# The exponentials' scores of an attention kernel: twelve products of 32 and 2 rows, or four products of 72 rows

## The chip, the cores and the metric

One core of a Trainium2 chip. The metric is device time in microseconds (us) of one launch: 1179.71 in the median of three runs (1178.32 to 1181.1). Lower is better.

## The reference, cut to what matters

One transformer layer on x of shape 2 x 1024 x 512: layer norm, attention with 32 heads of 16 columns, residual, layer norm, a feed-forward net (FFN) with ternary weights and rounded inputs, residual. The change concerns the scores and the softmax.

```python
q, k, v = (proj(w_q), proj(w_k), proj(w_v))        # (2, 32, 1024, 16) each
scores = jnp.einsum('bhqd,bhkd->bhqk', q, k) / jnp.sqrt(jnp.float32(D_K))
attn = jax.nn.softmax(scores, axis=-1)             # exp(scores - max over k) / sum
out = jnp.einsum('bhqk,bhkd->bhqd', attn, v)
```

All inputs are float32. The softmax subtracts each query's maximum, so the kernel forms the scores twice: once with queries on the partitions, to take the maximum along the keys, and once with keys on the partitions, to take the exponential and multiply with v.

## The kernel before, in words

**Steps and slots.** The attention is cut into 32 steps: batch b (2), half of the queries h (2, 512 each), group g of eight heads (4), and s (2), which picks every other head of the group. So a step has four heads (r = 0 to 3) and 512 queries. A step's maxima take eight slots (512 keys x 128 queries of all four heads each), its exponentials eight others (128 keys x 512 queries), its product with v eight (128 keys each). The main loop (L1400 to L1445) runs over slots T. In slot T stand the maxima of step T/8, the exponentials of the step that began LE = 10 slots earlier, and the product with v of the exponentials of one slot earlier. TensorE, VectorE, ScalarE, GpSimd and SyncE each work through their own instructions in the order in which this loop writes them.

**Numbers in two halves.** q and k are each split into a part hi that TensorE multiplies exactly and a rest lo. A tile kst of 128 rows holds for each of the four heads 32 rows: 16 of hi, 16 of lo. qst is a pair of tiles: in qst[0] both 16-row halves are q's hi, in qst[1] its lo. One product of 32 rows (kst with qst[0]) adds hi*hi and lo*hi, a second one (with qst[1]) the rest. Each head has its own quarter of TensorE's rows, so products of different heads can run at once.

**Maxima.** max_mm (L586) makes 8 such products a slot, two for each head, into two score tiles (psm, 128 x 1024 in PSUM, two heads each). max_reduce (L598) has VectorE reduce each of them to two columns of pm. After a step's last slot max_parts (L602) joins the parts on VectorE and splits the negative maximum into hi and lo columns of mcols; max_rows (L610) turns them into rows with four small products (psn) and ScalarE copies them to mrow (L617), in the second slot of the next step.

**Exponentials.** exp_mm (L621) makes for each head two products of 32 rows with kst and qst, and a third of 2 rows, ones against the maximum's two rows in mrow, that subtracts the maximum. That is 12 a slot. exponentials (L632) has ScalarE take exp of each score tile of two heads (pse) into e.

**The order in a slot.** scores (L637) interleaves the exponentials of one pair of heads with the maxima of the other pair, so that all four quarters of the rows are in use: ten products in a run. The slot is: mixed run; product with v (weigh_values, L655: for each head 128 keys x 32 columns against e, accumulated in pso over the step); short fill; second mixed run; max_rows if due; fill.

**Fills.** Everything else (layer norm, projections, output projection, FFN, quantization of the FFN's weights) are generators in a planner (class Fillers, L31). Each slot it runs those that are due, by costs written in the code (L1444), mostly one or two groups of matrix products. Tasks of kind "back" (normalise, L671; weight sums, L757; weight quantization, L796) advance one step at each call, two a slot.

**Buffers.** Score tiles come from one PSUM pool of three (ps_s), given out in turn: two maxima tiles and two exponential tiles a slot, and psn's. The product with v has a bank of its own, the fills another. In SBUF kst has three buffers, qst six (three pairs), e four.

**Transfers.** project_qk (L460) writes hi and lo of q and k to DRAM (qD, kD), in the layout that lets load_k and load_q (L566, L569) read a step's kst (512 KB) and qst (2 x 256 KB) five slots before the step's maxima. load_v (L575) reads v (512 KB). For the first two steps parts of kst and qst are copied from SBUF directly (L492 to L506) and q is not written to DRAM. Nearly all of these are issued on SyncE's queue, in order; the weights' raw loads (load_raw, L750) on GpSimd's.

**The end** (the_end, L1043) is the last quarter's output projection and FFN, in an order of its own, in tiles that are free by then.

```python
def exp_mm(n, i, j, ps, l):
    for r in (2 * j, 2 * j + 1):
        rows = slice(32 * r, 32 * r + 32)
        if l < 2:
            left, right = kst[n][rows, i * P : (i + 1) * P], qst[n][l][rows, :]
        else:
            rows = slice(32 * r, 32 * r + 2)
            left, right = onesr[rows, :], mrow[n][rows, :]
        nc.tensor.matmul(ps[:, r % 2, :], left, right, start=(l == 0), stop=(l == 2))
```

## Time and profile before

| | us |
|---|---|
| median of three runs | 1179.71 |
| lowest and highest run | 1178.32, 1181.1 |
| span of the profiled execution | 1179.7 |
| ScalarE, exponentials (L634), 512 of 1.023 | 522.7 |
| VectorE, reductions of the maxima (L600), 512 of 1.222 | 623.8 |
| TensorE, maxima (L590), 2048 | 369.5 |
| TensorE, exponentials' scores (L630), 2048 of 32 rows, 1024 of 2 | 367.6 + 203.9 |
| TensorE, product with v (L660), 2048 | 272.9 |
| data moved | 135.35 MB, mean 115 GB/s |

The times of lines are those of the page's costliest groups. On TensorE a group's time is the stretch in which it and no earlier product ran, since products overlap; so the place of a run is better read from the starts in the timeline. The product with v and other float32 products appear as two records each. The chain of work that ended last lies on TensorE for 81% of the span, with 25% on the exponentials' scores, 18% on the product with v and 9% on the maxima. DMA engines are busy 50 to 70% of the time in the first 320 us and mostly 20 to 40% later.

### The profile page before, as it was taken

How to read it: one execution, taken by the hardware profiler on the slowest of the kernel's cores; microseconds unless marked ns; L12 is line 12 of the kernel's file. 1: busy time of each engine (PE TensorE's matmuls, PEld its weight loads, DVE VectorE, ACT ScalarE, POOL GpSimd, SP SyncE). 2: the span in 40 equal slices, each digit the busy share in tenths (PEclk: the TensorE clock that was granted, in tenths of full speed). 3: DMA queues.
4: the chain of work that ended last, by engine and by line, in shares of the span. 5: the costliest groups of instructions: out<-in, count | busy, mean ns of one | idle time of the engine just before them, and what ended most of it. 6: DMA issues, size and time to landing. Idle time of an engine off the chain costs nothing.

```text
span 1179.7 us, 21990 instructions
## 1 busy us (share of the span) xinstructions
PE 1154.8 (98%) x8922; PEld 522.5 (44%) x8922; DVE 868.8 (74%) x1261; ACT 686.8 (58%) x878; POOL 264.1 (22%) x319
## 2 busy tenths in 40 slices
PE   8899999999999999999999999999999999999998
PEld 5454444544444444544444445444444433444344
DVE  6765577898876677788866665786988788888467
ACT  2058765556565556566665555465666555665746
POOL 3224336465501101221011011022110001220111
PEclk9999999999999999999999999999999999999999
DMA  5666765556623323443633324244442516362300
GB/s 157 174 183 194 249 197 176 172 190 197 194 93 96 103 55 110 113 95 77 94 86 121 124 59 147 84 130 138 84 97 60 89 53 83 58 81 55 79 9 37
DMA packets 97099, 135.35 MB, mean 115 GB/s; under 512 B 34829, under 2 KB 54285, under 8 KB 96997
## 3 DMA queue, kind: packets, MB, share of 16 engines
q1 hardware_dynamic: 87204, 105.75, 34.6%
q0 software_dynamic: 9792, 28.19, 7.7%
q8 instruction: 70, 1.15, 0.4%
q14 instruction: 33, 0.26, 0.1%
HBM read 89.25 MB, written 37.19 MB: 107 GB/s over the span
## 4 chain that ended last, share of the span: by engine, by line
PE 81%; DVE 5%; DMA 5%; issue 2%; POOL 2%; SPq 2%; ACT 2%; POOLq 0%; DVEq 0%; ACTq 0%
PE pse L630 25%; PE pso L660 18%; PE psm L590 9%; PE psv L533 4%; PE psk L476 4%; PE psy L847 4%; PE psq L476 4%; PE pu L937 2%; PE py L1006 2%; DVE pm L600 2%; PE pg L937 2%; DMA rden<-rD 1%; PE psn L613 1%; SPq L505 1%; PE end L1161 1%
## 5 line engine op out<-in xcount | busy, mean ns | idle before, releaser
L600 DVE TENSOR_REDUCE pm<-psm 128x2 f32<-128x1024 f32 x512 | 623.8, 1222 | 242.9 <-PE pse L630 146.0
L634 ACT ACTIVATE e<-pse 128x1024 f32<-128x1024 f32 x512 | 522.7, 1023 | 408.2 <-PE pse L630 307.3
L590 PE MATMUL psm<-kst,qst 32*128 32x512 f32 x2048 | 369.5, 444 | 7.3 <-DMA kst<-kD 3.8
L630 PE MATMUL pse<-qst,kst 32*128 32x512 f32 x2048 | 367.6, 442 | 3.9 <-DVE pm L600 3.1
L630 PEld LDWEIGHTS pse<-qst,kst 32*128 32x128 f32 x2048 | 149.2, 183 | 332.8 <-issue 199.7
L660 PE MATMUL pso<-e,v 128*32 128x512 f32 x2048 | 272.9, 605 | 0.0
L630 PE MATMUL pse<-mrow,onesr 2*128 2x512 f32 x1024 | 203.9, 396 | 0.0
L590 PEld LDWEIGHTS psm<-kst,qst 32*128 32x128 f32 x2048 | 151.3, 183 | 25.5 <-ACT e L634 10.8
L630 PEld LDWEIGHTS pse<-mrow,onesr 2*128 2x128 f32 x1024 | 94.5, 183 | 3.3
L951 POOL TENSOR_TENSOR g<-g 128x460 f32<-128x460 f32 (+1 forms) x36 | 34.7, 964 | 244.7 <-ACT g L947 237.4
L660 PEld LDWEIGHTS pso<-e,v 128*32 128x32 f32 x2048 | 40.4, 108 | 94.4 <-issue 93.7
L807 POOL TENSOR_SCALAR low<-raws,whalf 128x512 bf16<-128x512 f32 (+2 forms) x35 | 52.0, 1488 | 30.5 <-DMA raws<-in_wuT 8.1
L476 PE MATMUL psq<-xnT,wq 128*128 128x512 f32 x112 | 57.8, 626 | 0.0
L533 PE MATMUL psv<-wv,xnT 128*128 128x128 f32 x384 | 53.2, 285 | 0.0
L533 PEld LDWEIGHTS psv<-wv,xnT 128*128 128x128 f32 x384 | 45.9, 191 | 12.5 <-issue 11.7
L847 PE MATMUL psy<-wo,OT 128*128 128x512 f32 x96 | 49.6, 625 | 0.0
L476 PE MATMUL psk<-xnT,wk 128*128 128x512 f32 x96 | 49.5, 624 | 0.0
L699 POOL TENSOR_TENSOR OT<-po,rden 128x512 f32<-128x512 f32 x15 | 19.2, 1278 | 99.5 <-PE pse L630 52.8
L547 POOL DMA_DIRECT2D vD<-vst x30 | 16.7, 559 | 110.5 <-ACT vst L545 107.8
L909 POOL TENSOR_SCALAR xn<-x,mv,a 128x512 f32<-128x512 f32 x12 | 25.1, 2089 | 71.5 <-DVE a L885 71.5
L937 PEld LDWEIGHTS <-xqT 128*128 128x128 bf16 x288 | 22.4, 98 | 37.8 <-issue 23.8
L937 PE MATMUL pg<-wg,xqT 128*128 128x460 fp8e4 (+1 forms) x144 | 34.2, 360 | 0.0
(227 smaller groups left out, 945.1 us busy)
## 6 DMA issues: line engine op xcount, KB each, us to landing
v<-vD SPq DMA_DIRECT2D x32, 512.0 KB
kst<-kD SPq DMA_DIRECT2D x31, 512.0 KB
qst<-qD SPq DMA_DIRECT2D x60, 256.0 KB
vD<-vst POOLq DMA_DIRECT2D x30, 256.0 KB, 5.7
qD<-hi_q SPq DMA_DIRECT2D x28, 256.0 KB
qD<-lo_q SPq DMA_DIRECT2D x28, 256.0 KB
x<-in_x SPq DMA_DIRECT2D x20, 256.0 KB
rden<-rD SPq DMA_DIRECT2D x15, 256.0 KB
```

Source lines behind the costliest of these rows:

```text
L476: nc.tensor.matmul(ps, w[:, c, :], xnT[b, h][:, c, :], start=(c == 0), stop=(c == KC - 1))
L533: nc.tensor.matmul(ps[:, i * P : (i + 1) * P], xnT[b, half][:, c, i * P : (i + 1) * P], w[:, c, :], start=(c == 0), stop=(c == KC - 1),)
L590: nc.tensor.matmul(ps[:, r % 2, :], qst[n][l][rows, t * P : (t + 1) * P], kst[n][rows, kh * QB : (kh + 1) * QB], start=(l == 0), stop=(l = ...
L600: nc.vector.tensor_reduce(pm[n][:, t, kh, 2 * j : 2 * j + 2], ps, AX.X, ALU.max, negate=True)
L630: nc.tensor.matmul(ps[:, r % 2, :], left, right, start=(l == 0), stop=(l == 2))
L634: nc.scalar.activation(e, ps, AF.Exp, scale=SCALE)
L660: nc.tensor.matmul(acc[n][32 * r : 32 * r + 32, :], vt[n][:, i, r, :], e[r // 2][:, r % 2, :], start=(i == 0), stop=(i == NT - 1),)
L807: nc.gpsimd.tensor_scalar(low, w, h[:rows, m, 1:2], None, ALU.is_lt)
L847: nc.tensor.matmul(ps, OT[b, h, g][:, i * P : (i + 1) * P], wo[g], start=(g == 0), stop=(g == NG - 1),)
L909: nc.gpsimd.tensor_scalar(xn, xt, mean, a, ALU.subtract, ALU.mult)
L937: nc.tensor.matmul(ps, xT[:, c, :], w[:, c, n : n + size], start=(c == 0), stop=(c == KC - 1))
L951: nc.gpsimd.tensor_tensor(g2[j], g2[j], g2[j], ALU.mult)
```

## The change

The exponentials' scores of a head become one product. A tile kw of 72 rows holds for each head 64 rows of k (hi and lo, each twice) and 8 rows of zeros and ones; qm holds 64 rows of q (hi, hi, lo, lo in the order that pairs each with each) and 8 rows with the maxima of all four heads, of which the ones in kw pick the two of the head. So one product over 72 of the 128 rows gives a head's scores with the maximum subtracted; a slot has four, on the whole array, one after another.

Two tiles kw hold four slots of keys each; load_kw reads one (512 KB) four slots before its use. load_qm reads qm (512 KB) for a step while its maxima are formed. kD holds k's rows twice (each half of k is written with four transfers, not two), and the first q is written to qD as well. The maxima's rows go into qm: ScalarE copies 8 rows x 2048, one copy for each head side by side.

The order in a slot: the maxima of all four heads in one run; product with v; short fill; the exponentials' four products; fill; then max_rows, in the first slot of the next step and not the second.

To make room, kst has two buffers, qst four, e two, mcols one, and the raw weights and their helper tile use the FFN's tiles; two gaps in normalise are longer; the_end takes its tiles from other buffers.

```diff
--- before
+++ after
@@ -311,10 +307,10 @@
-    mcols = [const.tile([P, TQ, P], F32R, name=f"mcols{k}") for k in range(2)]
+    MROW = 64
+    mcols = const.tile([P, TQ, P], F32R, name="mcols")
     vst = [const.tile([P, 2, 4, 4, 32], F32, name=f"vst{k}") for k in range(1)]
-    for m in mcols:
-        nc.gpsimd.memset(m.bitcast(F32), 0.0)
+    nc.gpsimd.memset(mcols.bitcast(F32), 0.0)
     for v in vst:
@@ -413,12 +409,12 @@
     qD = {
-        (b, g, h): dram.tile([2, 8 * 32, QB], F32, name=f"qD_{b}_{g}_{h}")
+        (b, g, h): dram.tile([8 * 64, QB], F32, name=f"qD_{b}_{g}_{h}")
         for b in range(B)
     }
-    kD = {(b, g): dram.tile([8 * 32, S], F32, name=f"kD_{b}_{g}") for b in range(B) for g in range(NG)}
+    kD = {(b, g): dram.tile([8 * 64, S], F32, name=f"kD_{b}_{g}") for b in range(B) for g in range(NG)}
     vD = {
@@ -504,22 +500,21 @@
                 yield ("copied",)
-            if which == 0:
-                return
         queue = nc.gpsimd if fast and not first else nc.sync
             if which == 0:
-                dst = qD[b, g, h][l].rearrange("(e a d) q -> a e d q", a=2, d=16)
+                dst = qD[b, g, h].rearrange("(e l a d) q -> l a e d q", l=2, a=2, d=16)[l]
                 for a in range(2):
             else:
-                dst = kD[b, g].rearrange("(e l d) q -> l e d q", l=2, d=16)[l]
-                queue.dma_start(dst[:, :, h * QB : (h + 1) * QB], part.bitcast(F32))
+                dst = kD[b, g].rearrange("(e a l d) q -> l a e d q", a=2, l=2, d=16)[l]
+                for a in range(2):
+                    queue.dma_start(dst[a][:, :, h * QB : (h + 1) * QB], part.bitcast(F32))
             yield ("gap", 1)
         b, _, g, s = steps[n]
-        return kD[b, g].rearrange("(r s e) q -> s r e q", r=4, s=2)[s]
+        return kD[b, g].rearrange("(r s a e) q -> s a r e q", r=4, s=2, a=2)[s][0]
@@ -560,8 +555,8 @@
     def places(n):
-        kst[n] = sb.tile([P, S], F32R, tag="kst", name=f"kst_{n}", bufs=3)
-        qst[n] = [sb.tile([P, QB], F32R, tag="qst", name=f"qst_{n}_{l}", bufs=6) for l in range(2)]
+        kst[n] = sb.tile([P, S], F32R, tag="kst", name=f"kst_{n}", bufs=2)
+        qst[n] = [sb.tile([P, QB], F32R, tag="qst", name=f"qst_{n}_{l}", bufs=4) for l in range(2)]
@@ -569,8 +564,33 @@
         for l, q in enumerate(qst[n]):
-            rows = qD[b, g, h][l].rearrange("(r s e) q -> s r e q", r=4, s=2)[s]
+            rows = qD[b, g, h].rearrange("(r s l e) q -> s l r e q", r=4, s=2, l=2)[s][l]
             nc.sync.dma_start(q.bitcast(F32), rows)
+
+    kw = [const.tile([P, 4, QB], F32R, name=f"kw{k}") for k in range(2)]
+    qm = {}
+
+    def subtraction_rows():
+
+        pick = sp.tile([P, 4], F32, tag="rstd1", name="pick")
+        pairs = ident[:, MROW : MROW + 8].rearrange("p (r c) -> p r c", c=2)
+        nc.vector.tensor_reduce(pick, pairs, AX.X, ALU.add)
+        src = pick[MROW : MROW + 8, :].rearrange("p (r o) -> p r o", o=1)
+        for k in kw:
+            nc.vector.tensor_copy(k[MROW : MROW + 8, :, :], src.to_broadcast([8, 4, QB]))
+
+    def load_kw(n, p):
+
+        b, h, g, s = steps[n]
+        src = kD[b, g].rearrange("(r s e) q -> s e r q", r=4, s=2)[s][:, :, QB * p : QB * (p + 1)]
+        nc.sync.dma_start(kw[p][:64].bitcast(F32), src)
+
+    def load_qm(n):
+
+        b, h, g, s = steps[n]
+        qm[n] = sb.tile([P, 4, QB], F32R, tag="qm", name=f"qm_{n}", bufs=2)
+        src = qD[b, g, h].rearrange("(r s e) q -> s e r q", r=4, s=2)[s]
+        nc.sync.dma_start(qm[n][:64].bitcast(F32), src)
@@ -603,7 +623,7 @@
         nc.vector.tensor_tensor(m, p[:, :, 0, :], p[:, :, 1, :], ALU.min)
-        cols = mcols[n % 2].rearrange("p t (r c) -> p t r c", r=4)
+        cols = mcols[:, :, MROW : MROW + 8].rearrange("p t (r c) -> p t r c", r=4)
         nc.vector.tensor_copy(cols[:, :, :, 0], m)
@@ -611,44 +631,43 @@
             nc.tensor.matmul(
-                ps[:, t * P : (t + 1) * P], mcols[n % 2][:, t, :], identr, start=True, stop=True
+                ps[:, t * P : (t + 1) * P], mcols[:, t, :], identr, start=True, stop=True
             )
-        mrow[n] = sb.tile([P, QB], F32R, tag="mrow", name=f"mrow_{n}", bufs=2)
-        nc.scalar.copy(mrow[n], ps)
+        rows = ps[MROW : MROW + 8, :].rearrange("p (o q) -> p o q", o=1)
+        nc.scalar.copy(qm[n][MROW : MROW + 8, :, :], rows.to_broadcast([8, 4, QB]))
-    def exp_mm(n, i, j, ps, l):
+    def exp_mm(n, i, j, ps):
+        k = kw[i // TQ]
         for r in (2 * j, 2 * j + 1):
-            rows = slice(32 * r, 32 * r + 32)
-            if l < 2:
-                left, right = kst[n][rows, i * P : (i + 1) * P], qst[n][l][rows, :]
-            else:
-
-                rows = slice(32 * r, 32 * r + 2)
-                left, right = onesr[rows, :], mrow[n][rows, :]
-            nc.tensor.matmul(ps[:, r % 2, :], left, right, start=(l == 0), stop=(l == 2))
+            nc.tensor.matmul(
+                ps[:, r % 2, :],
+                k[: MROW + 8, r, (i % TQ) * P : (i % TQ + 1) * P],
+                qm[n][: MROW + 8, r, :],
+                start=True,
+                stop=True,
+            )
     def exponentials(n, i, j, ps):
-        e = sb.tile([P, 2, QB], F32, tag="e", name=f"e_{n}_{i}_{j}", bufs=4)
+        e = sb.tile([P, 2, QB], F32, tag="e", name=f"e_{n}_{i}_{j}", bufs=2)
         nc.scalar.activation(e, ps, AF.Exp, scale=SCALE)
-    def scores(exps, maxs):
-
-
-        es = [(*x, scores_psum(f"pse_{x[0]}_{x[1]}_{x[2]}")) for x in exps]
-        ms = [(*x, max_tile(*x)) for x in maxs]
-        for l in range(3):
-            for x in es:
-                exp_mm(*x, l)
-            if l or not es:
-                for x in ms:
-                    max_mm(*x, l - bool(es)) if l - bool(es) < 2 else None
-        for x in es:
-            exponentials(*x)
+    def maxima(n, i):
+
+        ms = [(n, i, j, max_tile(n, i, j)) for j in range(2)]
+        for l in range(2):
+            for x in ms:
+                max_mm(*x, l)
         for x in ms:
             max_reduce(*x)
+
+    def weights_of(n, i, j):
+
+        ps = scores_psum(f"pse_{n}_{i}_{j}")
+        exp_mm(n, i, j, ps)
+        exponentials(n, i, j, ps)
@@ -678,7 +697,7 @@
             nc.sync.dma_start(dD[:, s, :], p[16 * (1 - s) :: 32, :])
-        yield ("gap", 4)
+        yield ("gap", 6)
         k = 8 * QB // P
@@ -689,7 +708,7 @@
         nc.sync.dma_start(bass.AP(rD.tensor, rD.offset, [[k, P], [1, k]]), den)
-        yield ("gap", 3)
+        yield ("gap", 5)
         rden = sb.tile([P, QB], F32, tag="rden", name=f"rden_{n}", bufs=1)
@@ -747,10 +766,14 @@
+    loads = [0]
+
     def load_raw(m, i, name):
         c, n, rows, cols = parts[i]
-        t = sb.tile([P, 512], F32, tag="raw", name=f"{name}{m}_{c}_{n}", bufs=4)
+        k = loads[0] = loads[0] + 1
+        tag, cols_all = (("iq", FC * P // 2), ("inter", I))[k % 2]
+        t = sb.tile([P, cols_all], F32, tag=tag, name=f"{name}{m}_{c}_{n}", bufs=2)
         nc.gpsimd.dma_start(t[:rows, :cols], ap[c * P : c * P + rows, n : n + cols])
@@ -798,12 +821,13 @@
         raw = deque(load_raw(m, i, "raws") for i in range(2))
+        lows = sb.tile([P, FC, P], BF16, tag="iqT", name=f"low{m}", bufs=1).rearrange("p c t -> p (c t)")
         yield ("gap", 2)
             w = raw.popleft()[:rows, :cols]
-            low = sb.tile([P, 512], BF16, tag="low", name=f"low{m}_{i}", bufs=2)[:rows, :cols]
+            low = lows[:rows, 512 * (i % 2) : 512 * (i % 2) + cols]
             nc.gpsimd.tensor_scalar(low, w, h[:rows, m, 1:2], None, ALU.is_lt)
@@ -1118,17 +1142,18 @@
-        quad = [t.bitcast(BF16) for t in place("qst", [P, QB], TQ, 6)]
+        quad = [t.bitcast(BF16) for t in place("qst", [P, QB], TQ, 4)]
         xqs, xT = [q[:, :H] for q in quad], [q[:, H:].rearrange("p (c t) -> p c t", c=KC) for q in quad]
-        xns = place("raw", [P, 512], TQ, 4)
+        xns = place("x", [P, 512], TQ, 4)
         v = place("inter", [P, I], 2, 2)
         iq += [t.bitcast(BF16)[:, :I] for t in place("v", [P, NT * P], 2, 2)]
-        pairs = place("e", [P, 2, QB], 4, 4)
-        iqT = [t.bitcast(BF16)[:, : FC * P] for t in place("kst", [P, S], 3, 3)]
-        iqT.append(pairs.pop().rearrange("p j q -> p (j q)").bitcast(BF16)[:, : FC * P])
+        wide4 = [t for q in place("qm", [P, 4, QB], 2, 2) for t in (q[:, :2, :], q[:, 2:, :])]
+        pairs = place("e", [P, 2, QB], 2, 2) + wide4[:2]
+        iqT = [t.bitcast(BF16)[:, : FC * P] for t in place("kst", [P, S], 2, 2)]
+        iqT += [t.rearrange("p j q -> p (j q)").bitcast(BF16)[:, : FC * P] for t in wide4[2:]]
         g2 = [t[:, j, :] for t in pairs for j in range(2)]
@@ -1405,6 +1430,13 @@
+        if T == 0:
+            subtraction_rows()
+        if im == 4 and nm < NSTEP:
+            load_qm(nm)
+        n, p = divmod(T + 4 - LE, NT)
+        if 0 <= n < NSTEP and p % TQ == 0:
+            load_kw(n, p // TQ)
         n = T // NT + 1
@@ -1419,13 +1451,9 @@
             max_parts(nm - 1)
-        exps = [(ne, ie, j) for j in range(2)] if 0 <= ne < NSTEP else []
-        maxs = [(nm, im, j) for j in (1, 0)] if nm < NSTEP else []
-        mixed = bool(exps and maxs)
-        if mixed:
-            scores(exps[:1], maxs[:1])
-        elif exps:
-            scores(exps, [])
+        exps = 0 <= ne < NSTEP
+        if nm < NSTEP:
+            maxima(nm, im)
         if 0 <= nw < NSTEP:
@@ -1435,14 +1463,13 @@
         fill.run(100.0, short=True)
-        if mixed:
-            scores(exps[1:], maxs[1:])
-        elif maxs:
-            scores([], maxs)
-        if im == 1 and 0 < nm <= NSTEP:
-            max_rows(nm - 1)
+        if exps:
+            weights_of(ne, ie, 0)
+            weights_of(ne, ie, 1)
         share = min(max(fill.pace([w[4:] for w in ffns]), SHARE), MORE)
         left = fill.run(share + min(left, SHARE))
+        if im == 0 and 0 < nm <= NSTEP:
+            max_rows(nm - 1)
         feed()
```

Left out: lowrow, which nothing reads, goes, and the warm-up products read mcols under its new name.

More of the change, by code (lines that the diff above doesn't have):

```diff
@@ L301 @@
     ones = onesr.bitcast(F32)
-    lowrow = const.tile([P, 1], F32, name="lowrow")
-    nc.vector.memset(lowrow, -1.0)
-    for i in range(4):
-        nc.vector.memset(lowrow[32 * i : 32 * i + 16, :], 0.0)
     second = const.tile([P, 1], I32, name="second")
@@ L1288 @@
         nc.tensor.matmul(
-            ps[:, k % 2, :], onesr, mcols[0].rearrange("p t c -> p (t c)"), start=True, stop=True
+            ps[:, k % 2, :], onesr, mcols.rearrange("p t c -> p (t c)"), start=True, stop=True
         )
```

## The prediction

> **What bounds the kernel now.** I read the page's busy table first, then the timeline of TensorE in the middle of the run, then the prologue, then ScalarE's timeline at the end. TensorE is the bound, and not by a margin that a mean hides: it is busy 98% of the span.
>
> ```profile
> PE 1154.8 (98%) x8922; PEld 522.5 (44%) x8922; DVE 868.8 (74%) x1261; ACT 686.8 (58%) x878; POOL 264.1 (22%) x319
> ```
>
> One slot of the middle, on TensorE (start, length, line, operation, count):
>
> ```profile
> 606.81 0.51 PE L630 MATMUL pse<-qst,kst 32*128 32x512 f32 x2
> 606.82 0.50 PE L590 MATMUL psm<-kst,qst 32*128 32x512 f32 x2
> 607.14 0.40 PE L630 MATMUL pse<-qst,kst 32*128 32x512 f32 x2
> 607.16 0.40 PE L590 MATMUL psm<-kst,qst 32*128 32x512 f32 x2
> 607.38 0.40 PE L630 MATMUL pse<-mrow,onesr 2*128 2x512 f32 x2
> 607.70 1.06 PE L660 MATMUL pso<-e,v 128*32 128x512 f32 x8
> 608.70 0.50 PE L630 MATMUL pse<-qst,kst 32*128 32x512 f32 x2
> ...
> 609.60 1.12 PE L476 MATMUL psk<-xnT,wk 128*128 128x512 f32 x2
> 610.66 0.50 PE L630 MATMUL pse<-qst,kst 32*128 32x512 f32 x2
> ```
>
> The reader is to see starts, not lengths (matmuls overlap): mixed run 606.81 to 607.70, 0.89; product with v 1.00; second mixed run 0.90; fill 1.06; next slot. Over the whole trace the first mixed run of a slot has median 0.905 and mean 0.952, the second 0.908 and 0.931, the product with v 0.997. 246 slots have both runs; a slot lasts 4.18 in the mean.
>
> What the change puts in their place already stands in the prologue: a run of four heads' maxima alone, and full-array products of the same type and width (the last warm-up matmuls).
>
> ```profile
> 9.30 2.81 PE L1288 MATMUL warm<-mcols,onesr 128*128 128x512 f32 x11
> 11.95 0.27 PE L405 MATMUL psx<-identr,x 128*128 128x128 f32 x1
> ...
> 43.27 0.74 PE L590 MATMUL psm<-kst,qst 32*128 32x512 f32 x8
> 43.94 1.98 PE L476 MATMUL psk<-xnT,wk_first 128*128 128x512 f32 x4
> ```
>
> Eight maxima products take 0.67 to the next start. The warm-up matmuls from 9.62 to 11.95 are 0.233 apart.
>
> **TensorE's sum.** New slot: 0.667 + 4 x 0.233 = 1.600 against 0.905 + 0.908 = 1.813, so -0.213 x 246 = **-52**. That a product over 72 rows costs what one over 128 does is bounded by the warm-ups' 0.233 above and, below, by nothing but their 512 columns; I take 0.233. The old runs hold (0.047 + 0.023) x 242 = 17 us over their medians, waits for VectorE and ScalarE; I let half go with them, **-9**, since the tight new order will have its own.
>
> The Trainium skill speaks against this sum: "TensorE: Matmul & The Clock Gate", section "Measured speedup vs the span model", gives four-fold row packing 3.07 times a plain product's rate. By that, 20 packed products are 20 x 0.233 / 3.07 = 1.52 a slot and the new 8 packed and 4 plain 1.54, so nothing is won and my total would be about 57 us higher; the runs above (1.81, with their changes of tiling) speak for the rows.
>
> **The round trip through ScalarE, new.** Now the exponentials' products stand right behind the product with v, and the next product with v needs both exponentials. Before, the pair was split over the slot and a whole mixed run lay between. ScalarE's back-to-back exponentials, at the end where nothing else is left:
>
> ```profile
> 1105.42 3.87 ACT L634 ACTIVATE e<-pse 128x1024 f32<-128x1024 f32 x4 [0.55 <-PE pse L630]
> 1109.17 0.87 ACT L994 ACTIVATE iq<-inter,negmagic 128x688 bf16<-128x688 f32 x1
> ```
>
> Four in 3.87, two in 1.94 (the first 1.02, the next 0.92 on). The trip: product with v 1.00; first pair of products 0.23, and about 0.39 for the second to run through plus 0.1 to release ScalarE; 1.94; 0.06 to release TensorE: 3.72 from one product with v to the next. TensorE's own work is 0.667 + 0.997 + 0.933 + fill = 2.60 + fill, so it covers the trip only where the fill is 1.12 or more. Fills I measured as the slot less its runs: 0.88 where it is one FFN chunk, 1.06 for half a projection; 179 of 246 lie under 1.12, short by 33 us together (22 if the trip is 0.07 shorter, 47 if 0.08 longer). **+33.** Behind the waiting half of the product with v stand the exponentials' products and the fill, and nobody else is late for it.
>
> **Maxima's rows.** They now close the first slot of a step, and ScalarE copies 8 x 2048 instead of 128 x 512. The copy took 0.58 and 1024 columns take 1.02, so 2048 come to about 1.9. The rows take one of the three score buffers, and the next slot's first exponential product wants it 0.43 + 0.667 + 0.997 = 2.1 after they begin; it is free after 0.6 + 1.9 + 0.06 = 2.6, and later where an evacuation of the fill (0.58) stands ahead. Wait 0.4 to 1.0, I take 0.75, times 31: **+23.** Before, the copy had the fill to hide in.
>
> **VectorE.** Both reductions start 0.78 after the maxima and take 2.35 (prologue). The second exponential product reuses the first maxima's buffer, free at 0.78 + 1.23 + 0.06 = 2.07; TensorE reaches it at 0.667 + 0.997 + 0.466 = 2.13. So VectorE's lateness passes straight on, where it had half a slot to spare. Its other work is 0.84 a slot and has some 1.65 of room; 46 slots exceed that, by 24 us together. Most of those have a short fill, where the trip above is later anyway: **+6** (0 to 24).
>
> **Prologue.** SyncE's queue, before (start, length, issues):
>
> ```profile
> 27.46 0.72 SPq L517 DMA_DIRECT2D kD<-hi_k  x1
> 28.23 0.61 SPq L517 DMA_DIRECT2D kD<-lo_k  x1
> ...
> 36.58 2.43 SPq L505 DMA_DIRECT2D kst<-hi_k  x4
> ...
> 44.55 0.58 SPq L567 DMA_DIRECT2D kst<-kD  x1
> ```
>
> Step 0's second half of keys (36.58) is needed by slot 4 at 40.1, and step 1's keys land at 55.5 after a 3.8 stall. The change puts two more 256 KB writes of kD and four of qD ahead of the first, and two more of kD ahead of the second. Writes of this kind landed 4 to 8 us after issue, a pair in 5.5. Six at 1.3 each (256 KB on the 8 engines that their landings show, at 84 ns a 2 KB packet) are 8 us; slot 4 goes to about 48.5, slot 8 from 55.7 to about 64.5. **+9**, and 1 for TensorE's clock, which fell to 0.51 for 3.5 us after the old stall (window 57.2 to 60.7): **+10** (3 to 20). The two new copies on VectorE at slot 0 (2048 columns each, some 2 us) lie inside that wait.
>
> **DMA in the first 270 us.** Each step adds three 512 KB loads (two kw, one qm), each half of k two writes. The landing records show that kst and qst loads use the same four engines (1 MB a step, 10.5 us there), and that v, with all sixteen, lands on twelve after about 4 us and on those four after 10 to 15. From 59 to 325 us I count 226 us of packets on these four, 85%; the last qst landed 0.0 and 0.3 us ahead of steps 4 and 6, 5 to 8 ahead of the others. No row shows a load of 64 rows; v's is the nearest (512 KB, sixteen engines, 1.3 us each), a load like kst's on four the far end. With v's price the four get 24 x 1.35 + 10 x 1.34 = 45 us more: 271 in a stretch of 256. What is late next is kst and qst, then kw. **+5** if the queues only shift the two tight steps, up to 35 if they set the pace. Later steps have a load of 35 to 40% and 7 us to spare: nothing. On SyncE's queue each kw load waits for the last exponentials' product of the slot before it, four slots (17 us) ahead of its use; behind it stand kst and qst (needed five slots on), qm, v and normalise()'s small transfers, which waited on this queue for the same slots before.
>
> **End.** Slots without maxima have 2.1 a slot now where they have no fill (1106.25 to 1108.40 on TensorE); the trip makes that 3.72. By the order of instructions ten such slots are left, with seven fills under 1.8: about 45 us from the last maxima to the last stage instead of 36.7, of which 3.3 is FFN work that moved there from the loop: **+6** (0 to 9). The wider gaps in normalise() move only queue work.
>
> **Buffers, at nothing.** e has two instead of four: a pair is written only after the product with v that read it has passed on TensorE, which the trip above contains already. kst and qst keep two steps instead of three, and the step before last was last read eight slots earlier. mcols is read once a step. The raw weights stay four deep in the FFN's tiles, which are idle until the weights are done; the half tiles of low are two as before.
>
> **Sum.** -52 - 9 + 33 + 23 + 6 + 10 + 5 + 6 = +22; rounded down for waits that overlap, +20. The profiled span is 1179.7 and the median of the runs 1179.71, so nothing lies around it: **1200 us**.
>
> **Rivals.** 0.2% (2.4 us) is about what can be told from no change.
> - *TensorE's sum decides (faster).* One mechanism: the trip stays under TensorE's work, because the fills after it are long enough. It decides at fill 1.12; if the true trip is 3.5 or less the 33 vanish and most of the maxima rows' 23 with them. 1200 - 33 - 12 = 1155 or so. For it: 98% busy, ScalarE only 58%. Against: 179 short fills. Chance 0.20.
> - *The four busy engines set the pace of the first 300 us.* +35 instead of +5: 1230. For it: 0.0 us of slack in step 4. Against: DMA is 0.62 busy in the mean there. Chance 0.18.
> - *Gains and waits cancel.* Trip 22, copy hidden to 12, prologue 3: 1200 - 11 - 11 - 7 = 1171, up to 1188. Chance 0.08, of which 0.03 faster, 0.03 within 0.2%, 0.02 slower.
> - *It does not do what it says:* a 72-row product streams at 0.43, as the first warm-ups did (13 in 5.68). +0.8 x 256: 1400. Chance 0.02.
> - Forecast, 1188 to 1215: 0.52.
>
> The range reaches from the first rival to a little past the second, 1155 to 1240; some 0.15 lies outside (0.07 below the first, 0.06 above the second, 0.02 the last). Faster by over 0.2%: 0.20 + 0.03 = 0.23; within: 0.03; slower: 0.52 + 0.18 + 0.02 + 0.02 = 0.74.
>
> **What would show it.** Right: the exponentials' products 0.233 apart; TensorE idle before L660 for ScalarE and, once a step, before the exponentials' first product for the maxima's copy of 1.9; slots with one FFN chunk at 3.7; slot 8 beginning near 64. Wrong: slots of 3.5 with no wait before the product with v; idle time for kst, qst or kw beyond the prologue; products 0.43 apart.

## The result, and the profile after

The changed kernel takes **1293.27 us** in the median of five runs (1291.43 to 1306.48), 1.0989 times the time before (95% interval 1.0944 to 1.1035). The forecast was 1200 with a range of 1155 to 1240: the direction was right, the time lies far outside. The profiled execution took 1298.42, its span is 1296.6, and differences by stretch below are worked out from this span and the 1179.7 of before.

Lines of the page after (busy time by engine, the slices in tenths, the chain that ended last):

```profile
PE 1190.2 (92%) x6874; PEld 553.1 (43%) x6874; DVE 847.0 (65%) x1259; ACT 706.8 (55%) x878; POOL 267.3 (21%) x322
...
PE   8679968889989999999999999979999999999998
...
PEclk9888987989979999999999999989999999999999
DMA  5686875776576564687766665638785645574210
...
PE 50%; DMA 28%; ACT 6%; issue 6%; POOL 4%; DVE 3%; SPq 3%; POOLq 0%; ACTq 0%; DVEq 0%
```

Three things to see. TensorE has 2048 product records fewer and yet more busy time. Its clock, 9 or more tenths in every slice before, lies at 7 to 9 in the first third. And the chain, on TensorE for 81% before, is on DMA for 28%: a kernel bound by TensorE has become, in places, one bound by transfers.

Where the time went is read from the starts of the slots' products with v: both traces have 256 of them, eight a step. This table (us) gives the length of stretches of the same work, cut at a step's first product with v:

| stretch | before | after | difference |
|---|---|---|---|
| start to the first product with v | 67.7 | 84.6 | +16.9 |
| steps 0 to 7 | 269.4 | 332.3 | +62.9 |
| steps 8 to 19 | 398.3 | 405.1 | +6.8 |
| step 20 | 38.3 | 50.4 | +12.1 |
| steps 21 to 30 and the last up to its last slot | 350.6 | 361.6 | +11.0 |
| from there to the end | 55.4 | 62.6 | +7.2 |

So 63 of 117 us are lost in the first eight steps and 12 in a single later one; steps 8 to 19, the quiet stretch, cost 7. Steps 0 to 7, before and after (length; busy time of PE, PEld, DVE, ACT, POOL; TensorE's clock; DMA share; GB/s):

```profile
67.70:337.10 269.40, 267.08 (x2166) 126.10 (x2164) 202.74 (x252) 173.41 (x247) 124.41 (x146) 1.00 0.62 194
84.60:416.90 332.30, 288.08 (x1656) 141.81 (x1652) 196.86 (x253) 177.99 (x245) 123.51 (x144) 0.90 0.70 199
```

TensorE, idle for 2 us of this stretch before, is idle for 44, and its clock falls to 0.90. TensorE's waits over the whole span (us in total, times, longest):

```profile
PE pse L644 <- DVE pm L620: 24.0, 17, 7.3
PE psm L610 <- DMA qst<-qD: 22.8, 5, 11.8
PE pse L644 <- ACT qm L637: 14.0, 30, 1.2
PE psm L610 <- DMA kst<-hi_k: 10.5, 1, 10.5
PE psm L610 <- DMA kst<-kD: 6.3, 1, 6.3
```

A slot of the quiet stretch, on TensorE (start, length, line, count):

```profile
667.78 0.74 PE L610 MATMUL psm<-kst,qst 32*128 32x512 f32 x8
668.45 1.06 PE L679 MATMUL pso<-e,v 128*32 128x512 f32 x8
669.44 1.20 PE L644 MATMUL pse<-qm,kw 72*128 72x512 f32 x4
670.48 0.83 PE L1030 MATMUL py<-wd,iqT 128*128 128x512 fp8e4 x3
671.24 0.84 PE L610 MATMUL psm<-kst,qst 32*128 32x512 f32 x8
672.00 1.31 PE L679 MATMUL pso<-e,v 128*32 128x512 f32 x8
673.25 0.73 PE L644 MATMUL pse<-qm,kw 72*128 72x512 f32 x2
674.67 0.74 PE L644 MATMUL pse<-qm,kw 72*128 72x512 f32 x2 [0.68 <-DVE pm L620]
```

The maxima take 0.67 and the exponentials' products are 0.232 apart, as forecast; only the first behind the product with v takes 0.339 (the change goes from products on four column tiles to products on the whole array). The second product with v is held up inside: 672.00 to 673.25 is 1.25 where the first took 0.99. That this is the round trip through ScalarE is tested by e9 below.

Now the largest stall of the first eight steps, on TensorE, and what SyncE's queue did:

```profile
182.97 1.06 PE L528 MATMUL psv<-wv,xnT 128*128 128x128 f32 x8
195.82 0.80 PE L610 MATMUL psm<-kst,qst 32*128 32x512 f32 x4 [11.80 <-DMA qst<-qD]
200.13 0.80 PE L610 MATMUL psm<-kst,qst 32*128 32x512 f32 x4 [3.51 <-DMA qst<-qD]
```

```profile
180.66 3.03 SPq L568 DMA_DIRECT2D qst<-qD  x2
183.79 1.62 SPq L699 DMA_DIRECT2D dD<-po  x2
185.46 0.64 SPq L593 DMA_DIRECT2D qm<-qD  x1
186.14 1.14 SPq L453 DMA_DIRECT2D wq<-in_wqT  x1
187.33 6.48 SPq L586 DMA_DIRECT2D kw<-kD  x1
200.62 0.33 SPq L703 DMA_DIRECT2D den<-dD  x1
```

The two loads of qst were issued at 180.7 and 183.2 and their last landing records stand at 195.7 and 200.1, 15 and 17 us later, exactly where TensorE goes on. A transfer's landing shows in the trace as a row of records, the updates of its semaphore. Each of these two has five, 1 at once and 4 late; so have kst's and even dD's, which are 8 KB and also take 16.5 us. wq, with sixteen records but in the same queue behind them, lands after 16.9; vD (185.2) and raws (186.3), with sixteen records through GpSimd's queue, after 7 and 8.

### The profile page after: what moved, and what is told of

It reads as the page before. It is cut to its first block, busy times and chain, and to the rows that moved or that the text cites. A ratio compares the mean times of both kernels' runs of the same rounds, so it can differ in the third digit from the quotient of the medians.

```text
span 1296.6 us, 18168 instructions
## 1 busy us (share of the span) xinstructions
PE 1190.2 (92%) x6874; PEld 553.1 (43%) x6874; DVE 847.0 (65%) x1259; ACT 706.8 (55%) x878; POOL 267.3 (21%) x322
## 4 chain that ended last, share of the span: by engine, by line
PE 50%; DMA 28%; ACT 6%; issue 6%; POOL 4%; DVE 3%; SPq 3%; POOLq 0%; ACTq 0%; DVEq 0%
PE pse L644 13%; PE pso L679 12%; DMA qst<-qD 7%; PE psm L610 7%; DMA rD<-den 4%; DMA rden<-rD 4%; DMA kD<-lo_k 3%; PE psy L871 3%; ACT qm L637 3%; PE py L1030 2%; DMA qD<-lo_q 2%; PE psq L472 2%; PE psk L472 2%; DMA iqT<-iq 2%; DVE pm L620 2%
## 5 line engine op out<-in xcount | busy, mean ns | idle before, releaser
L620 DVE TENSOR_REDUCE pm<-psm 128x2 f32<-128x1024 f32 x512 | 602.5, 1219 | 308.7 <-PE psm L610 308.5
L654 ACT ACTIVATE e<-pse 128x1024 f32<-128x1024 f32 x512 | 497.9, 1021 | 425.8 <-PE pse L644 422.3
L644 PE MATMUL pse<-qm,kw 72*128 72x512 f32 x1024 | 320.9, 432 | 38.9 <-DVE pm L620 24.0
L679 PE MATMUL pso<-e,v 128*32 128x512 f32 x2048 | 313.5, 617 | 5.5 <-DMA v<-vD 3.4
L644 PEld LDWEIGHTS pse<-qm,kw 72*128 72x128 f32 x1024 | 173.1, 192 | 293.6 <-issue 142.4
L610 PE MATMUL psm<-kst,qst 32*128 32x512 f32 x2048 | 210.1, 456 | 45.6 <-DMA qst<-qD 22.8
L610 PEld LDWEIGHTS psm<-kst,qst 32*128 32x128 f32 x2048 | 87.9, 187 | 168.1 <-issue 68.6
L637 ACT CAST qm<-psn 8x2048 fp32r<-8x2048 f32 x32 | 59.4, 1857 | 27.1 <-PE psn L633 26.6
L984 DVE TENSOR_TENSOR inter<-pu,g 128x460 f32<-128x460 f32 (+1 forms) x36 | 22.8, 633 | 25.9 <-PE pu L961 25.9
L1030 PE MATMUL py<-wd,iqT 128*128 128x512 fp8e4 (+1 forms) x132 | 34.9, 407 | 2.4 <-DMA iqT<-iq 1.6
```

The lines of the kernel that those rows point to most:

```text
L610: nc.tensor.matmul(ps[:, r % 2, :], qst[n][l][rows, t * P : (t + 1) * P], kst[n][rows, kh * QB : (kh + 1) * QB], start=(l == 0), stop=(l = ...
L620: nc.vector.tensor_reduce(pm[n][:, t, kh, 2 * j : 2 * j + 2], ps, AX.X, ALU.max, negate=True)
L637: nc.scalar.copy(qm[n][MROW : MROW + 8, :, :], rows.to_broadcast([8, 4, QB]))
L644: nc.tensor.matmul(ps[:, r % 2, :], k[: MROW + 8, r, (i % TQ) * P : (i % TQ + 1) * P], qm[n][: MROW + 8, r, :], start=True, stop=True,)
L654: nc.scalar.activation(e, ps, AF.Exp, scale=SCALE)
L679: nc.tensor.matmul(acc[n][32 * r : 32 * r + 32, :], vt[n][:, i, r, :], e[r // 2][:, r % 2, :], start=(i == 0), stop=(i == NT - 1),)
```

## The experiments

**First: three theories of the 63 us, and the prologue.** A: four of the sixteen DMA engines have too much to carry. B: SyncE's queue. C: the new order on TensorE.

*e1, the keys and queries on sixteen engines:*

```diff
-        nc.sync.dma_start(kst[n][:, first:].bitcast(F32), step_k(n)[:, :, first:])
+        for r in range(4):
+            nc.sync.dma_start(kst[n][32 * r : 32 * r + 32, first:].bitcast(F32), step_k(n)[r, :, first:])
...
-            nc.sync.dma_start(q.bitcast(F32), rows)
+            for r in range(4):
+                nc.sync.dma_start(q[32 * r : 32 * r + 32, :].bitcast(F32), rows[r])
```

> The changed kernel, but each step's keys (kst) and queries (qst) are loaded with one transfer for each head (four of 128 KB and eight of 64 KB, 32 rows each) in place of three transfers whose slowest dimension is the four heads. Bytes and packet sizes stay. Theory A (four of the sixteen DMA engines carry kst and qst and a share of everything else, and have more work than time until about 420 us; every transfer waits for them): the five-record landings go, kst and qst land after 4 to 8 us instead of 14 to 18, and of the 63 us lost in steps 0 to 8, the 12 at step 20 and the 5 at step 23 some 55 to 75 come back: 1220 to 1240. Theory B (SyncE's queue is the limit, by its order and its number of transfers under way): nine more transfers a step make it worse, 1295 to 1320. Theory C (the new order on TensorE, or the bytes as such): 1285 to 1300.

Measured **1229.17** (1224.54 to 1229.2), ratio 1.0402 (1.0361 to 1.0444): 64 us less from the same bytes in the same data packets. The landing records of kst and qst number 16, and in steps 0 to 7 qst's last one comes after 5.4 us in the median instead of 19.0, kst's 7.9 instead of 16.2, dD's, which keeps its five records, 1.8 instead of 15.5. Step 20 of the changed kernel, then steps 0 to 7 and step 20 of this run:

```profile
822.00:872.40 50.40, 41.41 (x206) 17.27 (x202) 28.20 (x50) 18.78 (x21) 1.08 (x2) 0.90 0.45 120
```

```profile
77.30:364.80 287.50, 268.60 (x1654) 133.18 (x1650) 196.20 (x253) 177.42 (x245) 124.44 (x146) 0.99 0.84 234
...
764.80:802.70 37.90, 37.74 (x202) 16.21 (x198) 28.18 (x50) 18.60 (x21) 1.07 (x2) 1.00 0.56 141
```

The DMA share rises (0.70 to 0.84) and the time falls: the mean of sixteen engines hid that four of them had more to carry than the rest. B, by which more transfers on the queue cost time, and C fall for the 64 us.

*e2, without the added traffic:*

```diff
-        nc.sync.dma_start(kw[p][:64].bitcast(F32), src)
+        if n == 0:
+            nc.sync.dma_start(kw[p][:64].bitcast(F32), src)
...
-        nc.sync.dma_start(qm[n][:64].bitcast(F32), src)
+        if n < 2:
+            nc.sync.dma_start(qm[n][:64].bitcast(F32), src)
...
-                for a in range(2):
+                for a in range(1 if b or g else 2):
```

> The changed kernel without most of the added traffic: kw is loaded for step 0 only, qm for steps 0 and 1 only, and k is written twice only in the first group; all later exponentials use step 0's keys and step 0's or 1's queries (the output is not the reference's). TensorE's order and products, VectorE's and ScalarE's work stay. Theory A (backlog on four DMA engines, made by the added traffic) and theory B (SyncE's queue) agree: 63 + 17 less, 1205 to 1225, and the prologue's 17 us stay. Theory C (the new order on TensorE): 1285 to 1300.

Measured 1235.44 (1228.5 to 1243.41); its profiled span is 1226.7, e1's 1227.4. Ten us above what A and B expected of it, since both forgot that steps 0 to 7 would still lose 15 us (284.1 against 269.4), of which e8 shows a part to be VectorE's order. Taking the added transfers away and spreading the old ones bring nearly the same: neither alone is the fault, but the two together. This run also takes transfers off SyncE's queue, so by itself it does not tell engines from queue.

*e3, the prologue's order:*

```diff
-    now(keys[0])
-    now(queries)
     now(firsts[1])
-    now(keys[1])
+    upto(keys[1], "copied")
+    upto(queries, "copied")
+    now(keys[0])
+    now(keys[1])
     load_k(1)
+    now(queries)
```

> The changed kernel with one reordering ahead of the loop: the copies of the second half of step 0's keys and of step 1's queries come before the first writes of kD and qD on SyncE's queue. If the prologue's 17 us are these writes ahead of the copies (theory P): slot 4 no longer waits and the first product with v comes 6 to 12 us sooner; if nothing swallows it, 1281 to 1287. If four DMA engines set the pace up to step 8 (theory A), part of it is lost again there: 1285 to 1293.

Measured 1297.38 (1294.32 to 1305.32). A miss: slot 4 no longer waits (10.5 before), but slot 8 waits 13.3 instead of 6.3 for step 1's keys, since eight writes of kD now stand together ahead of their load, and that load takes 9.1 on four engines. The first product with v comes at 85.1 instead of 84.6: the wait moved.

*e4, the kernel before, spread:* the edit of e1 in the kernel before.

> The kernel before with kst and qst loaded by one transfer a head as in the first run. Theory A says that the backlog did not bind there beyond the wait of 3.8 us for step 1's keys in the prologue: 1172 to 1180. Theory B: nine more transfers a step, 1180 to 1195.

Measured **1175.34** (1173.99 to 1177.83), ratio 0.9959 (0.9941 to 0.9977): faster than both kernels. The wait of 3.8 us for step 1's keys goes, and of the other stretches above none changes by more than 2 us. So four engines were not the limit before, beyond that wait.

**Second: engines or queue, and what is left.** No issue on SyncE's queue, in the traces of before, of after, of e1 and of e2, has more than seven earlier transfers under way (they use eight semaphores in turn). That gave a theory D: not the engines are full, but eight places with landings of 15 to 19 us make a rate.

*e5, kw and qm on GpSimd's queue:*

```diff
-        nc.sync.dma_start(kw[p][:64].bitcast(F32), src)
+        nc.gpsimd.dma_start(kw[p][:64].bitcast(F32), src)
...
-        nc.sync.dma_start(qm[n][:64].bitcast(F32), src)
+        nc.gpsimd.dma_start(qm[n][:64].bitcast(F32), src)
```

> The changed kernel (loads of kst and qst on four engines, as it was) with the loads of kw and qm issued on GpSimd's queue and not on SyncE's. Theory A (the four engines have more packets than time): they still carry all of it, 1285 to 1305. Theory D (SyncE's queue never has more than eight transfers under way, the next waits until the one eight back has landed, and the slow landings of kst and qst, 14 to 19 us, make that a rate; the four engines are slow but not full): three of the step's transfers leave that queue, most of the 64 us go, 1225 to 1250.

Measured 1317.64 (1313.38 to 1320.53), worse than A expected. Steps 0 to 7 take 319.8, where the changed kernel takes 332.3 and e1 287.5, so 12 of those 45 us come back. The landings get no faster with places free: qst's last record comes after 23.1 us in the median, 19.0 in the changed kernel. The run loses elsewhere (the first product with v comes at 93.4, and steps 14 and 15 lose 27 us against before, and TensorE waits 15.7 us for iqT in all); what issuing on GpSimd costs was not separated, so the 12 is no upper bound.

The traces settle D more directly. An issue that has to wait for a place starts 0.02 us after the transfer eight back has landed. In steps 0 to 7 of the changed kernel such waits are 12 and add up to 10 us; in e1, which is 45 us faster there, they are 44 and 47 us. So the places are not what e1 relieved. Something else on this queue does fall with e1: issues that last over 1.5 us (kw's at 187.33 takes 6.48, though the transfer eight back had landed at 183.1) are 32 in the changed kernel's stretch, 119 us together, and 9 in e1's, 20 us. What ends such an issue, the trace does not show.

*e6, k written once, and the prologue's order on top of e1:*

```diff
-        nc.sync.dma_start(kw[p][:64].bitcast(F32), src)
+        for a in range(2):
+            nc.sync.dma_start(kw[p][32 * a : 32 * a + 32].bitcast(F32), src)
...
-                for a in range(2):
-                    queue.dma_start(dst[a][:, :, h * QB : (h + 1) * QB], part.bitcast(F32))
+                queue.dma_start(dst[:, :, h * QB : (h + 1) * QB], part.bitcast(F32))
```

> The first run (kst and qst by one transfer a head), and k is written to DRAM once, not twice: kw's two halves are both read from the one copy, with a transfer each; and the copies of the second half of step 0's keys and of step 1's queries come ahead of the first writes, as in the third run. If what is left of the prologue's loss is kD's doubled writes (theory P2: step 1's keys wait for eight writes in place of four), the first product with v goes from 77.3 to 63 to 68 and the total to 1214 to 1220. If the four writes of q or the three new loads hold it, 75 to 78 and 1226 to 1232.

Measured 1220.99 (1218.01 to 1223.68). The first product with v comes at 73.1, between the two expectations: 4 us of the prologue come back with the doubled writes and their order, 5 stay.

*e7, the round trip taken out by another order* (with a third tile e):

```diff
             maxima(nm, im)
+        if exps:
+            weights_of(ne, ie, 0)
         if 0 <= nw < NSTEP:
...
         feed()
-        fill.run(100.0, short=True)
         if exps:
-            weights_of(ne, ie, 0)
             weights_of(ne, ie, 1)
+        fill.run(100.0, short=True)
```

> The first run with another order in a slot: maxima, the exponentials' products of one pair of heads, product with v, those of the other pair, fill; with a third buffer for e (room: the residual is read straight into the tile of its sum, mcols has 72 columns). Theory R (the round trip through ScalarE costs TensorE 0.19 a slot inside the product with v and the maxima, as the traces of steps 9 to 20 show): these waits go, 0.15 to 0.2 x 246, 1180 to 1195, less what the maxima's rows then cost more (up to 10 more). Rival (VectorE's reductions and the three score buffers bind at once behind it, since a buffer is used again after three tiles): 1215 to 1230.

Measured 1292.27 (1279.68 to 1298.37): a miss for both. The waits inside the product with v do go (a median of 0.996, as before), but a step's second slot now stands like this:

```profile
447.70 0.52 PE L612 MATMUL psm<-kst,qst 32*128 32x512 f32 x4
449.85 0.73 PE L646 MATMUL pse<-qm,kw 72*128 72x512 f32 x2 [1.63 <-ACT qm L639]
450.51 1.06 PE L681 MATMUL pso<-e,v 128*32 128x512 f32 x8
451.51 0.73 PE L646 MATMUL pse<-qm,kw 72*128 72x512 f32 x2
```

The wide copy of the maxima's rows, right ahead of the products that need its buffer, costs 40 us over 28 steps; every pair of products now begins with a change of tiling (0.34 from its first product to its second, twice a slot, and 0.33 from the pair to the product with v), and the clock of steps 8 to 19 falls to 0.97. Theory R is not refuted by this, only not separated.

*e8, the quantization behind the reductions:*

```diff
             yield ("gap", 1)
+            while not fill.after_maxima:
+                yield ("gap", 1)
             nc.vector.scalar_tensor_tensor(
```

> The first run with VectorE's part of the quantization of the weights put only behind a slot's reductions and never just ahead of the next slot's. Theory V (steps 3 to 8 lose 16 to 18 us against the kernel before, in the first and in the second run alike, since an operation that waits for GpSimd stands ahead of the reductions): 10 to 14 less, 1214 to 1220. Rival (VectorE simply has more work than time in these slots): 1225 to 1230.

Measured 1217.41 (1214.35 to 1223.23), 12 less than e1, as expected. In steps 0 to 7 TensorE's wait for VectorE's reductions is 2.7 us, and VectorE's waits for GpSimd's low (19 us there in e1's steps 2 to 7) are gone.

**Third: the round trip and the rows by themselves.**

*e9, shorter exponentials* (half of each weight tile e then holds ones, so the output is not the reference's):

```diff
-        e = sb.tile([P, 2, QB], F32, tag="e", name=f"e_{n}_{i}_{j}", bufs=2)
-        nc.scalar.activation(e, ps, AF.Exp, scale=SCALE)
+        e = e_two[j]
+        nc.scalar.activation(e[:, :, : QB // 2], ps[:, :, : QB // 2], AF.Exp, scale=SCALE)
```

> The first run (keys and queries by one transfer a head), with exponentials of only the first 256 of each head's 512 queries (the rest of e holds ones, so the output is not the reference's); TensorE's work, order and buffers stay, two tiles e are kept for good. It takes about half the time off each exponential and so 0.9 us off the round trip. Theory R (the round trip binds, 0.19 a slot in the product with v and the maxima, and 3.8 a slot at the end): the waits for ScalarE inside the product with v go, the last step's product with v takes 21 to 23 us in place of 28, and the total falls to 1170 to 1190. Rival (the new products and their changes of tiling simply take what the old ones took, and the trip is no more than its visible idle time): 1205 to 1222.

Measured **1188.69** (1180.12 to 1194.16), just inside what R expected. From step 9 to step 31 the kernel before takes 732.4, e1 738.5 and this run 706.6. But e1's trace holds an accident there. In steps 25 and 27 its clock falls to half with hardly a wait ahead of it (0.39 and 0.56 us in the 3.4 us before), and 5.1 us of busy time are lost:

```profile
960.00:962.00 2.00, 2.00 (x10) 0.20 (x8) 2.00 (x2) 0.89 (x1) 0.00 (x0) 0.50 0.00 0
962.00:964.00 2.00, 2.00 (x9) 1.28 (x6) 0.21 (x1) 0.67 (x1) 0.00 (x0) 0.50 0.00 0
```

e2 and e8, with the same order on TensorE and no such fall in these steps, take 733.4 and 733.3. Against them the trip is 27 us in 22 steps, 0.15 a slot (against e1 it would be 32, 0.18). Steps 0 to 7 show no gain (288.7, e1 287.5): 13.5 us of busy time are lost to a lower clock there, 4.0 in e1. So the trip's price for all slots, in the table below, is extrapolated from these 22 steps. At the end, slots without a fill show it bare; the changed kernel first, then this run:

```profile
1220.93 1.97 PE L679 MATMUL pso<-e,v 128*32 128x512 f32 x8 [0.70 <-ACT e L654]
1222.83 1.19 PE L644 MATMUL pse<-qm,kw 72*128 72x512 f32 x4
1224.73 1.97 PE L679 MATMUL pso<-e,v 128*32 128x512 f32 x8 [0.71 <-ACT e L654]
```

```profile
1116.17 1.54 PE L686 MATMUL pso<-e,v 128*32 128x512 f32 x8 [0.28 <-ACT e L661]
1117.64 1.21 PE L647 MATMUL pse<-qm,kw 72*128 72x512 f32 x4
1119.13 1.54 PE L686 MATMUL pso<-e,v 128*32 128x512 f32 x8 [0.28 <-ACT e L661]
```

From one product with v to the next it is 3.80 in the changed kernel (the forecast's trip: 3.72) and 2.96 here.

*e10, the rows' copies on GpSimd:*

```diff
-        nc.scalar.copy(qm[n][MROW : MROW + 8, :, :], rows.to_broadcast([8, 4, QB]))
+        nc.scalar.copy(q[:, 0, :], ps[MROW : MROW + 8, :])
+        nc.gpsimd.tensor_copy(q[:, 1:, :], q[:, :1, :].bitcast(F32).to_broadcast([8, 3, QB]))
```

> The first run, with ScalarE copying the maxima's 8 rows once (8 x 512) and GpSimd making the other three copies from there. If the wide copy costs TensorE 0.6 to 0.9 a step at the next slot's first exponential product, as the prediction had it (+23 in all): 15 to 23 less, 1206 to 1214. Rival (ScalarE was late for the round trip in those slots anyway, or GpSimd comes too late with the copies): 1220 to 1232.

Measured 1228.95 (1226.81 to 1230.33), the same as e1 and inside the rival's range. The stretches differ: from step 9 to step 31 this run takes 724.2, 9 less than e8 and e2 (0.41 a step, below the 0.6 to 0.9 expected; TensorE's waits for the wide copy in these steps are 9.2 in both). In steps 0 to 7, where GpSimd also quantizes the weights, it loses 10 against e1, and a chain can be read off: GpSimd copies, is late with low, VectorE waits for low with the reductions behind it, TensorE waits for these. Most of the 10 shows as a lower clock: 12.8 us of busy time are lost to it here, 4.0 in e1. Another 6 are lost in the prologue (first product with v at 83.0 instead of 77.3), where the copy stands ahead of GpSimd's writes of kD and VectorE waits 6.3 for one of these. From this run:

```profile
222.59 1.46 POOL L640 CAST qm<-qm 8x1536 fp32r<-8x1536 f32 x1
...
224.68 1.56 POOL L834 TENSOR_SCALAR low<-raws,whalf 128x512 bf16<-128x512 f32 x1
...
226.27 0.75 DVE L836 SCALAR_TENSOR_TENSOR wg<-raws,whalf,low 128x512 fp8e4<-128x512 f32 x1 [3.29 <-POOL low L834]
...
226.94 2.35 DVE L622 TENSOR_REDUCE pm<-psm 128x2 f32<-128x1024 f32 x2
...
228.21 0.96 PE L647 MATMUL pse<-qm,kw 72*128 72x512 f32 x2 [1.95 <-DVE pm L622]
```

*e11, the parts together:* the edits of e1, e6, e8 and e10.

> Together: keys and queries by one transfer a head, k written once, the copies ahead of the first writes, the quantization behind the reductions, and the rows' copies on GpSimd. If the parts add up (8 + 12 + 10 to 20 off 1229): 1190 to 1200. If they share their waits: 1205 to 1215. No theory makes it faster than the kernel before, since the end (14) and the rest of the prologue stay.

Measured 1207.07 (1204.29 to 1211.72), ratio 1.0228 (1.0207 to 1.0249). The parts share their waits, and the copy on GpSimd costs in the prologue again: the first product with v comes at 81.9, in e6 at 73.1, and TensorE stands 9.0 us for VectorE, which waits for a write of kD issued behind the copy. No version with the change reaches the time before.

*e12, the prologue's order in the kernel before:* the edits of e4 and e3.

> The kernel before with keys and queries by one transfer a head, as in the fourth run (1175), and with the copies of step 0's second half of keys and of step 1's queries ahead of the first writes. Theory P2 (writes ahead of the copies hold the prologue): at most the 1 to 2 us of idle that is left there, 1173 to 1176. Rival (the later writes delay step 1's keys): 1176 to 1182.

Measured 1179.23 (1175.7 to 1188.59), ratio 0.9989 (0.9971 to 1.0008). The first product with v comes at 66.3, in e4 at 63.2: the rival was right, the later writes delay step 1's keys. e4 stays the fastest version.

## Why the prediction was wrong, point by point

| step of the prediction | forecast | measured | from |
|---|---|---|---|
| TensorE's sum, with the old waits | -61 | about -47 | e9, steps 9 to 30: -25.8, with 7.9 of the rows' waits still in it, so -0.19 a slot x 246 |
| round trip through ScalarE | +33 | about +37 | e8 (or e2) and e9: 0.15 a slot x 246 |
| maxima's rows | +23 | about +13 | e8 (or e2) and e10: 0.41 a step x 31 |
| VectorE | +6 | about +10 | e1 and e8, steps 0 to 7 |
| prologue | +10 | +9.6 | e1, first product with v |
| DMA | +5 | +69 | spans of the changed kernel and of e1 (64 between the medians) |
| end | +6 | +14 | last step's last slots +6.8, and behind it +7.2 |

The right column adds up to 106, against 117 between the spans. Some 5 of the difference are the falls of e1's clock in steps 25 and 27, which make the DMA row too small; the rest is open. Steps 0 to 7 take 277.8 even in e8, 8 more than before. The terms were each read from another pair of runs, so none is good to better than a few us.

**The step that failed is the term for DMA in the first 270 us, priced at +5, with nothing for later steps.** In its place the runs show +69, or 64 between the medians. It had the right suspect, four engines, and the right place. It failed in three ways.

- *Packets were priced undisturbed.* The step counted 226 us on the four engines and added 45, at 84 ns for 2 KB. In steps 0 to 7 a 2 KB packet took 97 ns in the mean before and 119 after, a 4 KB packet of the page's queue q1 211 and 207. The trace does not name engines, so what the four carried is an estimate from these means: with all packets of kst and qst on four engines and the others even on sixteen, 250 of 269 us before and 320 of 332 after. So the slack of 15% that the step saw was not there. The price alone is not the loss: e1 has the same 119 ns, 0.84 of 287.5 us on each engine, and lacks the 64 us.
- *The sum was weighed as if 271 in 256 could be shifted into slack.* Rival 2 had it, at +35, with a chance of 0.18. Its price was short as well, because a stall costs twice: TensorE's clock falls. In steps 0 to 7 of the changed kernel TensorE stands idle 44 us (before: 2), and of its busy time 25 us are lost to a lower clock (0 before). e1 has 19 and 4: of the 45 us that it wins there, 25 are idle time and 21 clock. The forecast allowed 1 us for the clock.
- *The 7 us to spare in later steps looked at the loads alone.* The four engines delay everything that uses them. In step 20 it is xr, an operand that VectorE adds to the output projection (this view is of the changed kernel):

```profile
838.55 2.36 DVE L620 TENSOR_REDUCE pm<-psm 128x2 f32<-128x1024 f32 x2 [2.33 <-PE psm L610]
849.42 0.69 DVE L887 TENSOR_TENSOR x<-psy,xr 128x512 f32<-128x512 f32 x1 [8.51 <-DMA xr<-in_x]
850.02 2.35 DVE L620 TENSOR_REDUCE pm<-psm 128x2 f32<-128x1024 f32 x2
```

xr was issued at 836.26 behind dD (4.19 on the queue) and landed 13.1 us later, behind kst, qst and dD on the four engines; VectorE waited, the reductions stood behind, and TensorE stood for 7.3 us, which the waits put down to VectorE. e1 has no such wait, and step 20 takes 37.9 instead of 50.4.

The rest of the prediction held in kind. TensorE's sum: the products are 0.232 apart and a slot gains 0.19, where the forecast had 0.213 and half of the old waits; a change of tiling costs 0.11 behind the product with v, and is given back ahead of the maxima (fill of two projection products to the maxima 0.952, to the old exponentials 1.056). The Trainium skill's figure in the prediction ("TensorE: Matmul & The Clock Gate", section "Measured speedup vs the span model") would have had this gain at nothing; e9 sides with the rows of the trace. The round trip: 3.72 forecast, 3.80 seen, and +37 for +33. In steps 9 to 30 it shows in e8 and not in e9 as 0.13 a slot in the product with v and 0.05 in the maxima behind it, of which 0.03 is lost again at the exponentials' products behind; the forecast had nobody else late for it. The maxima's copy: 1.9 forecast, 1.857 in the page; the wait for it was 0.41 a step, not 0.75. VectorE: +10 for +6, but by another path: VectorE's waits for GpSimd's low, 5.4 us in steps 0 to 7 before, are 18.9 in e1, and the reductions stand behind them (e8). The prologue's +10 held only with spread loads: 7 more came with step 1's keys on four engines (slot 8 began at 71.05, not 64.5; 63.3 in e1). The end: the trip in slots without a fill was right, but FFN work and the output projection also moved behind the last slot.

Of the forecast's signs of being right, slot 8 near 64 failed (71.05). It named "idle time for kst, qst or kw beyond the prologue" as a sign of being wrong, and that is what the waits show (qst 22.8). The sum of all other steps, by the forecast's own numbers, is +17; by the runs it is some +48 (117 less 69), of which e11 takes back a part.

## What to carry to other kernels

Before adding transfers, count on how many DMA engines each lands, not the mean share: the records of one landing tell it (here 1 + 4 against 16), and an outermost dimension of four in the address pattern can make four engines the bound while the page shows 0.7. Price the load of the fullest engines by packets from a busy stretch, and take all that queues behind it, the small transfers and those of other stages too; then add the clock, which fell behind the longer stalls here. Where an order is made tighter, list for each wait on the second engine (here VectorE's for GpSimd) what it used to hide behind.

## What the runs showed of the hardware

- Transfers with a slowest dimension of four land with four late records (qst: 15 and 17 us in the stall shown) and hold up others. On the number of engines, the Trainium skill, "DMA: Bandwidth & Descriptors", section "🎯 Rules for kernel authors", states that such a transfer is confined to at most as many engines as its outermost dimension has entries. The records agree (1 + 4 against 16), and e1 gives the price here, 64 us; before, the same pattern cost 4 (e4).
- An 8 KB transfer (dD) takes 14.5 us in the median of the later steps behind such loads, and 1.7 in e1.
- TensorE's clock after a stall (windows of the changed kernel around the one shown above: length, busy times, clock third from the end):

```profile
184.00:188.00 4.00, 0.03 (x1) 0.00 (x0) 0.06 (x1) 1.18 (x3) 2.67 (x5) 1.00 0.53 171
188.00:192.00 4.00, 0.00 (x0) 0.00 (x0) 0.00 (x0) 0.00 (x0) 0.00 (x0) 0.59 1.02 275
...
200.00:204.00 4.00, 3.87 (x16) 1.68 (x17) 2.52 (x3) 0.00 (x0) 0.00 (x0) 0.50 0.55 168
204.00:208.00 4.00, 4.00 (x8) 2.08 (x7) 0.00 (x0) 1.94 (x2) 0.00 (x0) 0.50 0.91 311
208.00:212.00 4.00, 3.72 (x24) 1.84 (x23) 1.93 (x2) 1.86 (x1) 0.00 (x0) 0.85 0.08 25
```

  It is at half some 4 to 5 us into the stall and comes back some 9 us after TensorE works without a break again (200.1), so 15 us of waiting cost several more. A long stall is not needed: e1's falls in steps 25 and 27 came after waits of 0.39 and 0.56 us.
- On SyncE's queue at most eight transfers are under way, and an issue that waits for a place starts 0.02 us after the transfer eight back has landed. This explains little here: such waits are 10 us in steps 0 to 7 of the changed kernel and 47 in e1, which is faster.
